# A two-layer graph network on one core: first layer from gathered bf16 rows of h, sums kept by span, products of zeros on TensorE

## The chip, the core and the metric

The kernel runs on one core of a Trainium2 chip. A core has TensorE (PE), VectorE (DVE), ScalarE (ACT), GpSimd (POOL) and SyncE (SP), each with its own queue, and 16 DMA engines. The metric is the device time of one execution in microseconds.

## The reference

`x` is 12500 nodes by 64. There are 212500 edges, sorted by target; `src`, `dst`, a type of 16 and 8 attributes each.

```python
h = relu(layernorm(x))
# layer one: 16 relations
msg = sum_r (h[src] * (etype == r)) @ weight[r]
x = x + segment_sum(msg, dst)
h = relu(layernorm(x))
# layer two: W1 is 136 x 64, W2 is 64 x 64
m = relu(concat(h[src], h[dst], attr) @ W1 + b1) @ W2 + b2
x = x + segment_sum(m, dst)
```

## The kernel before

Nodes are held as 98 blocks of 128 (`x3`, resident in SBUF). Edges are cut into tiles of 128, four tiles to a group: 1661 tiles with edges, 416 groups. As edges are sorted, the targets of a group lie in a window of `W` = 64 nodes that starts at the group's first target.

**Front** (lines 143 to 236). `x` is loaded in stretches of 16 blocks over SP and ACT in turn (line 111). Several tables are derived from `dst`, `src` and the types (lines 169 to 209), among them `flag`, which says whether the sorted path may be taken; with the data used here it is. Then `layer_norm` (lines 131 to 137) runs over 14 blocks at a time, PE transposes (L216) and multiplies each node's h with all 16 matrices (L223), DVE and ACT evict (L234, L235), and SP stores `rel_rows`, 1024 floats per node (L236).

**Layer one** (loop at line 351, in `in_order`). Per group, `gather` (L278) issues on POOL one indirect DMA per tile: 128 rows of 64 floats from `rel_rows`, at index source x 16 + type, into one of 8 buffers `rows_of`. `targets` (L289) lets DVE build a one-hot of each edge's place in the window. `add_sums` multiplies rows and one-hots on PE into the PSUM tile `pa` (L310, two buffers) and DVE adds it into `acc` at the window's column (L312); `acc` holds the sums of all nodes as columns. The windows' columns are loaded into registers for eight groups at a time (L298). When a span of four blocks can get no more sums (`finished`), `second_products` transposes it (L327), adds it to `x` (L328), normalises, and stores two tables: `a_rows` (h times the first 64 rows of W1) and `b_rows` (h times the next 64 rows, plus b1) (L349).

**Layer two** (loop at line 377). It needs all of `a_rows`. Per group POOL gathers `a_rows[src]`; SP loads the group's window of `b_rows` (L391, 64 rows, above 8 rows of W1) and its attributes (L394, under the one-hot); ACT builds a transposed one-hot of the targets by `relu(1 - |dst - w|)` (L396, L402); one f32 product per tile gives b and attribute terms (L405); DVE adds the gathered rows (`z`, L407), ACT applies relu (`hid`, L409), and `add_sums` runs again with a 65th row of ones for b2. `results` multiplies a finished span with W2 (L367), adds `x` (L369) and stores.

The order within each engine is that of the program, as the tile framework emits it; an engine that waits holds everything queued behind it.

Of the kernel before, what the change touches and what calls it, by code (L numbers as in the profile page):

```python
# [37 lines left out]
P = 128  # L38
# [7 lines left out]
NB = -(-N // P)  # L46
NT = 1664
# [5 lines left out]
G = 4  # L53
W = 64
# [4 lines left out]
BS = 4  # L59
GS = 17  # L60
SLACK = 2
NCHK = (NGR - SLACK) // GS
RG = 8

# [18 lines left out]
def gnn_kernel(  # L83
    ctx: ExitStack, tc, x, src, dst, etype, attr, src_t, dst_t, typ_t, attr_t, first, last, w_rel, w1, b1, w2, b2, out
# [7 lines left out]
    rel_rows = dram.tile([NB * P, R * D], F32, name="rel_rows")  # L92
    a_rows = dram.tile([NB * P, D], F32, name="a_rows")
    b_rows = dram.tile([NW, D], F32, name="b_rows")
    rel_table = rel_rows.rearrange("n (r d) -> (n r) d", r=R)
# [12 lines left out]
    XL = 16  # L108
    for i, b0 in enumerate(range(0, NB - 1, XL)):
        b1_ = min(b0 + XL, NB - 1)  # L110
        (nc.sync, nc.scalar)[i % 2].dma_start(
            x3[:, b0:b1_, :], x[b0 * P : b1_ * P].rearrange("(b p) d -> p b d", p=P)
        )
    nc.scalar.dma_start(x3[:tail, NB - 1, :], x[(NB - 1) * P :])
    flag = keep.tile([1, 1], I32, name="flag")
    first_row = keep.tile([1, NGR], I32, name="first_row")
    row_i = keep.tile([P, NT], I32, name="row_i")
    src_i = keep.tile([P, NT], I32, name="src_i")
    local = keep.tile([P, NT], F32, name="local")

    neg_w = keep.tile([W, NGR], F32, name="neg_w")
    none_row = float((NB * P - 1) * R)

    def layer_norm(pool, b0, nb, name):

        st = pool.tile([P, nb, 6], F32, name=f"{name}_st")
        mv = pool.tile([P, nb, 2], F32, name=f"{name}_mv")
        rs = pool.tile([P, 2, nb], F32, name=f"{name}_rs")
        h = pool.tile([P, nb, D], F32, name=f"{name}_h")
        for k in range(nb):  # L130
            V.bn_stats(st[:, k, :], x3[:, b0 + k, :])  # L131
        for k in range(nb):
            V.bn_aggr(mv[:, k, :], st[:, k, :])
        S.activation(rs[:, 0, :], mv[:, :, 1], AF.Sqrt, bias=eps, scale=1.0)  # L134
        V.reciprocal(rs[:, 1, :], rs[:, 0, :])
        for k in range(nb):
            V.tensor_scalar(
                h[:, k, :], x3[:, b0 + k, :], mv[:, k, 0:1], rs[:, 1, k : k + 1], op0=ALU.subtract, op1=ALU.mult
            )
        return h  # L140


    with ExitStack() as c1:
# [3 lines left out]
        ps3 = c1.enter_context(tc.tile_pool(name="p1ps3", bufs=3, space=PSUM))  # L147

        wrel = big.tile([P, R, D], F32, name="wrel")
        for k in range(2):  # L150
            nc.scalar.dma_start(wrel[k * D : (k + 1) * D], w_rel.rearrange("r i o -> i r o"))


        seq = big.tile([P, NT], I32, name="seq")
        nxt = big.tile([P, NT], I32, name="nxt")
        nc.sync.dma_start(seq, dst[:EP].rearrange("(p j) -> p j", p=P))
        nc.sync.dma_start(nxt, dst[1 : EP + 1].rearrange("(p j) -> p j", p=P))
        ends = big.tile([P, 2, NGR], I32, name="ends")
        nc.scalar.dma_start(ends[:, 0, :], first.unsqueeze(0).to_broadcast([P, NGR]))
        nc.scalar.dma_start(ends[:, 1, :], last.unsqueeze(0).to_broadcast([P, NGR]))  # L160
        nc.scalar.dma_start(first_row, first.unsqueeze(0))
        nc.sync.dma_start(src_i, src_t)
        typ_i = big.tile([P, NT], I32, name="typ_i")
        nc.sync.dma_start(typ_i, typ_t)
        dst_i = big.tile([P, NT], I32, name="dst_i")
        nc.sync.dma_start(dst_i, dst_t)

        bad = big.tile([P, NT + NGR + NCHK], F32, name="bad")
        V.tensor_tensor(bad[:, :NT], nxt, seq, op=ALU.is_lt)
        ends_f = big.tile([P, 2, NGR], F32, name="ends_f")  # L170
        V.tensor_copy(ends_f, ends)
        V.scalar_tensor_tensor(
            bad[:, NT : NT + NGR], ends_f[:, 1, :], -float(W), ends_f[:, 0, :], op0=ALU.add, op1=ALU.is_ge
        )
        want = big.tile([P, NCHK], F32, name="want")
        G_.iota(
            want, pattern=[[BS * P, NCHK]], base=BS * P, channel_multiplier=0, allow_small_or_imprecise_dtypes=True
        )

        at = ends_f[:, 0, GS + SLACK :: GS]  # L180
        nchk = at.shape[1]
        V.memset(bad[:, NT + NGR :], 0.0)
        V.tensor_tensor(bad[:, NT + NGR : NT + NGR + nchk], at, want[:, :nchk], op=ALU.is_lt)
        sums = big.tile([P, 2], F32, name="sums")
        V.memset(sums[:, 1:2], 1.0)
        V.tensor_reduce(sums[:, 0:1], bad, axis=AX.X, op=ALU.add)
        pf = ps1.tile([1, 1], F32, name="hT_p")
        T.matmul(pf, lhsT=sums[:, 0:1], rhs=sums[:, 1:2], start=True, stop=True)
        V.tensor_copy(flag, pf)

        ok = big.tile([P, NT], F32, name="ok")
        typ_f = big.tile([P, NT], F32, name="typ_f")
        V.tensor_copy(typ_f, typ_i)
        V.tensor_scalar(ok, typ_f, 0.0, None, op0=ALU.is_ge)
        V.scalar_tensor_tensor(ok, typ_f, float(R), ok, op0=ALU.is_lt, op1=ALU.mult)
        V.scalar_tensor_tensor(typ_f, src_i, float(R), typ_f, op0=ALU.mult, op1=ALU.add)
        V.scalar_tensor_tensor(typ_f, typ_f, -none_row, ok, op0=ALU.add, op1=ALU.mult)
        V.tensor_scalar(row_i, typ_f, none_row, None, op0=ALU.add)  # L200
        V.tensor_tensor(
            local.rearrange("p (g k) -> p g k", k=G),
            dst_i.rearrange("p (g k) -> p g k", k=G),
            bc(ends_f[:, 0, :], 2, G, [P, NGR, G]),
            op=ALU.subtract,
        )
        row_w = big.tile([W, 1], F32, name="row_w")
        G_.iota(row_w, pattern=[[0, 1]], base=0, channel_multiplier=1, allow_small_or_imprecise_dtypes=True)
        V.tensor_scalar(neg_w, ends_f[:W, 0, :], row_w, -1.0, op0=ALU.add, op1=ALU.mult)

        LB = 14
        for b0 in range(0, NB, LB):
            h = layer_norm(wk, b0, LB, "r")
            for b in range(0, LB, 2):
                hT_p = ps1.tile([P, P], F32, name="hT_p")
                T.transpose(hT_p, h[:, b : b + 2, :].rearrange("p k d -> p (k d)"), ident)  # L216
                hT = wk.tile([P, P], F32, name="hT")
                S.activation(hT, hT_p, AF.Relu)  # L218
                pr = [ps3.tile([P, R * D], F32, name="pr") for _ in range(2)]
                half = R * D // 2  # L220
                for j in range(2):
                    for k in range(2):
                        T.matmul(  # L223
                            pr[k][:, j * half : (j + 1) * half],
# [16 lines left out]
    def in_order():  # L241
        with ExitStack() as c2:
# [20 lines left out]
            for t in bwin:  # L263
                nc.scalar.dma_start(t[W:, :], w1[2 * D :])
# [557 lines left out]
```

## Time and profile before

| | |
|---|---|
| median of 11 runs | 5148.47 us (5140.68 to 5157.12) |
| profiled execution | 5147.21 us, span 5145.3 us |
| busy | PE 1814.5, DVE 837.3, ACT 753.4, POOL 3143.2 us |
| first gather, last gather of layer one | 243.5 us, 2593.4 us |
| first gather of layer two, last | 2612.3 us, 5116.5 us |

In a group line of the profile, "x1661 | 1571.2, 946 | 1021.4" is 1661 instructions, 1571.2 us busy, 946 ns each, 1021.4 us of idle time just before them. "remote" is a signal whose sender the profile doesn't name, "issue" is time in which nothing visible was waited for. The granted clock is TensorE's share of its full clock. An f32 matmul shows as two records.

### The profile page before, as it was taken

The numbers are of one execution on the slowest core, as the hardware profiler recorded it, in microseconds if no ns is written. First come the engines' busy times: TensorE is split into PE (matmuls) and PEld (weight loads), VectorE is DVE, ScalarE is ACT, GpSimd is POOL, SyncE is SP. The second block draws the span as 40 slices with busy tenths as digits, with TensorE's granted clock in tenths as the row PEclk, the third lists the DMA queues.
The fourth block names the chain that finished last, engine by engine and source line by source line (L and its number), as shares of the span: only waits on it lengthen the run. The fifth ranks groups of instructions, "written<-read, shape, count | busy, mean of one in ns | idle before, by whom it ended". The sixth has DMA issues, their size and how long they took to land. (4 is left out here: it accounts for less than half of the span.)

```text
span 5145.3 us, 37992 instructions
## 1 busy us (share of the span) xinstructions
PE 1814.5 (35%) x10948; PEld 1598.3 (31%) x10948; DVE 837.3 (16%) x2995; ACT 753.4 (15%) x1575; POOL 3143.2 (61%) x3331
## 2 busy tenths in 40 slices
PE   4522122212122112222135444444445444444445
PEld 1211111111121112111124444444444444444445
DVE  5411111111111111111111111111111111111111
ACT  2300000000000000000012222222222222222222
POOL 0066666666666666666656666666666566666665
PEclk9855555555555555555555555555555555555555
DMA  6611111111111111111112222222222232222222
GB/s 227 258 25 27 26 25 27 26 26 27 26 26 28 25 26 28 26 25 27 25 34 46 53 45 52 55 46 54 45 56 50 45 60 47 52 45 54 53 45 43
DMA packets 219120, 249.35 MB, mean 48 GB/s; under 512 B 145655, under 2 KB 145912, under 8 KB 215576
## 3 DMA queue, kind: packets, MB, share of 16 engines
q0 software_dynamic: 106304, 109.07, 11.4%
q1 hardware_dynamic: 103282, 135.08, 9.7%
q10 hardware_dynamic: 9318, 2.69, 0.3%
q8 instruction: 91, 1.49, 0.1%
q14 instruction: 125, 1.02, 0.1%
HBM read 185.55 MB, written 61.02 MB: 48 GB/s over the span
## 5 line engine op out<-in xcount | busy, mean ns | idle before, releaser
L278 POOL DMA_INDIRECT rows_of<-rel_rows,row_i x1661 | 1571.2, 946 | 1021.4 <-issue 415.9
L278 POOL DMA_INDIRECT rows_of<-a_rows,src_i x1661 | 1570.9, 946 | 952.1 <-issue 469.7
L310 PE MATMUL pa<-oh,rows_of 128*64 128x64 f32 x3322 | 434.4, 314 | 1419.4 <-DVE acc L312 702.4
L405 PE MATMUL pab<-bwin,ohT 72*128 72x64 f32 x3322 | 794.5, 421 | 286.8 <-issue 118.3
L405 PEld LDWEIGHTS pab<-bwin,ohT 72*128 72x128 f32 x3322 | 753.4, 332 | 299.2 <-remote 100.7
L310 PEld LDWEIGHTS pa<-oh,rows_of 128*64 128x64 f32 x3322 | 371.3, 217 | 1484.1 <-DVE acc L312 721.6
L310 PE MATMUL pa<-oh,hid 128*65 128x64 f32 x3322 | 459.7, 319 | 952.1 <-ACT hid L409 771.4
L310 PEld LDWEIGHTS pa<-oh,hid 128*65 128x65 f32 x3322 | 405.3, 229 | 985.2 <-ACT hid L409 794.2
L312 DVE TENSOR_TENSOR acc<-acc,pa 64x64 f32 (+1 forms) x832 | 178.5, 215 | 3142.5 <-remote 2426.2
L402 ACT ACTIVATE ohT<-off 64x512 f32<-64x512 f32 x416 | 253.9, 620 | 838.6 <-issue 402.1
L289 DVE TENSOR_TENSOR oh<-local,iota_p 128x256 f32<-128x256 f32 x832 | 338.1, 407 | 44.0 <-remote 43.0
L409 ACT ACTIVATE hid<-z 128x256 f32<-128x256 f32 x416 | 169.1, 408 | 1042.1 <-DVE z L407 800.7
L396 ACT ACTIVATE off<-dst_bc,neg_w 64x512 f32<-64x512 int32 x416 | 282.6, 708 | 15.1 <-DMA dst_bc<-in_dst 12.5
L407 DVE TENSOR_TENSOR z<-pab,rows_of 128x256 f32<-128x256 f32 x416 | 173.3, 421 | 664.7 <-remote 342.0
L134 ACT ACTIVATE s_rs<-s_mv,eps 128x4 f32<-128x4 f32 (+1 forms) x25 | 7.4, 297 | 1762.4 <-DVE s_st L131 1086.0
L223 PE MATMUL pr<-wrel,hT 64*128 64x512 f32 x392 | 111.1, 690 | 69.9 <-ACT hT L218 69.9
L339 PE MATMUL pab<-w1ab,hT 64*128 64x128 f32 x196 | 40.3, 498 | 227.4 <-issue 146.7
L339 PEld LDWEIGHTS pab<-w1ab,hT 64*128 64x128 f32 x196 | 25.6, 308 | 236.0 <-issue 151.0
L367 PE MATMUL pT<-w2b,acc 65*128 65x64 f32 x196 | 48.0, 426 | 106.2 <-DVE acc L312 87.0
L234 DVE COPY rows<-pr 128x512 f32<-128x512 f32 x98 | 63.8, 685 | 97.6 <-issue 75.0
L367 PEld LDWEIGHTS pT<-w2b,acc 65*128 65x128 f32 x196 | 44.0, 329 | 109.6 <-DVE acc L312 89.4
L235 ACT COPY rows<-pr 128x512 f32<-128x512 f32 x98 | 57.7, 588 | 130.2 <-DVE rows L234 113.1
(57 smaller groups left out, 350.0 us busy)
## 6 DMA issues: line engine op xcount, KB each, us to landing
dst_bc<-in_dst SPq DMA_DIRECT2D x52, 1024.0 KB
rel_rows<-rows SPq DMA_DIRECT2D x49, 1024.0 KB
rows_of<-rel_rows,row_i POOLq DMA_INDIRECT x1661
rows_of<-a_rows,src_i POOLq DMA_INDIRECT x1661
ohT<-in_attr_t SPq DMA_DIRECT2D x416, 16.0 KB
bwin<-b_rows SPq DMA_DIRECT2D x416, 16.0 KB
a_rows<-ab SPq DMA_DIRECT2D x24, 128.0 KB
b_rows<-ab SPq DMA_DIRECT2D x24, 128.0 KB
```

The lines of the kernel that those rows point to most:

```text
L223: T.matmul(pr[k][:, j * half : (j + 1) * half], lhsT=hT[k * D : (k + 1) * D, :], rhs=wrel[k * D : (k + 1) * D, j * R // 2 : (j + 1) * R // ...
L278: G_.indirect_dma_start(out=t[:, i, :], out_offset=None, in_=table, in_offset=bass.IndirectOffsetOnAxis(ap=idx[:, k : k + 1], axis=0),)
L289: V.tensor_tensor(oh[:, :n, :], bc(local[:, g * G : g * G + n], 2, W, [P, n, W]), bc(iota_p, 1, n, [P, n, W]), op=ALU.is_equal,)
L310: T.matmul(pa[:rows], lhsT=lhs(i), rhs=oh[:, i, :], start=(i == 0), stop=(i == n - 1))
L312: V.tensor_tensor(to, to, pa[:rows], op=ALU.add)
L339: T.matmul(pab.rearrange("p s d -> p (s d)"), lhsT=hT[i * D : (i + 1) * D, :], rhs=w1ab[i * D : (i + 1) * D].rearrange("i k o -> i (k o)") ...
L367: T.matmul(po[:, k, :], lhsT=acc[:, (b0 + k) * P : (b0 + k + 1) * P], rhs=w2b, start=True, stop=True)
L396: S.activation(off, dst_bc[:, (g % RG) * G * P : (g % RG + 1) * G * P], AF.Abs, bias=neg_w[:, g : g + 1],)
L402: S.activation(ohT[:W, :], off, AF.Relu, bias=1.0, scale=-1.0)
L405: T.matmul(pz[:, i, :], lhsT=ohT[:, i * P : (i + 1) * P], rhs=bw, start=True, stop=True)
L407: V.tensor_tensor(z[:, :n, :], pz[:, :n, :], a_of[:, :n, :], op=ALU.add)
L409: S.activation(r[:, :n, :D], z[:, :n, :], AF.Relu)
```

## The change

**Front.** The table of relations and its products go. Instead each node's relu(h) is split into three bf16 parts (together about 24 bits) and stored as a row of 192 bf16, `h_rows`. `x` comes on SP alone, in eight uneven chunks; GpSimd takes the two subtractions of the split. The tables that need whole passes over the edges move into the loop of layer one, in eight parts (`load_part`, `codes`).

**Layer one.** A tile's gather takes 128 rows of `h_rows`, at the source alone, into one of 12 buffers (as in layer two). ACT builds per tile a one-hot over 16 relations x 12 places (a window of `WT` = 12 nodes per tile), in bf16. Six bf16 products per tile (three parts, two halves of the relations) give sums of h by relation and node, and DVE adds them per tile into a table that covers a span of two blocks and 128 nodes ahead; two such tables take turns. When a span is done, `finish` multiplies its table with the 16 matrices (eight f32 products of 128 x 128 by 64 per block) and goes on as `second_products` did; its steps are spread over the following tiles. The last two blocks are finished one by one. `b_rows` is stored as three bf16 parts.

**Beside it.** `attributes` splits the edge attributes into bf16 parts for layer two, in DRAM.

**Layer two.** Windows have 40 nodes, the one-hots and both operands of the products at L405 are bf16: 120 rows of b parts, and 72 rows of attributes against `w1c_9`. `prepare`, `hidden` and `add_up` run for three successive groups at a time. Sums lie in two span tables.

**Products of zeros.** `keep_busy` issues bf16 products of a zero tile, 512 columns wide: two after each tile of layer one but the last few groups, seven in `prepare` and seven in `add_up` of layer two.

The core of the diff:

```diff
-W = 64
+W = 40
+WT = 12
+FRONT = (6, 14, 14, 14, 14, 14, 12, 10)
+FILL_N = 512
+FILL1 = 2
+FILL2 = 14
...
+        def rows_of_sources(b0, nb):
+            h = layer_norm(wk, b0, nb, "r")
+            parts = wk.tile([P, nb, 3, D], BF16, name="parts", bufs=3)
+            rest = wk.tile([P, nb, D], F32, name="rest")
+            S.copy(parts[:, :, 0, :], h)
+            G_.tensor_tensor(rest, h, parts[:, :, 0, :], op=ALU.subtract)
+            S.copy(parts[:, :, 1, :], rest)
+            G_.tensor_tensor(parts[:, :, 2, :], rest, parts[:, :, 1, :], op=ALU.subtract)
+            nc.sync.dma_start(
+                h_rows[b0 * P : (b0 + nb) * P, :].rearrange("(b p) c -> p b c", p=P),
+                parts.rearrange("p b k d -> p b (k d)"),
+            )
...
+        for k, nb in enumerate(FRONT):
+            rows_of_sources(sum(FRONT[:k]), nb)
+            if k == 5:
+                checks()
...
-                t = wk.tile([P, G, D], F32, name="rows_of", bufs=8)
+                t = wk.tile([P, G, width], dtype, name=f"rows{width}", bufs=12)
...
+            def relations(code, k, n):
+                off = wk.tile([P, G, RW], BF16, name="off_r")
+                oh = wk.tile([P, G, RW], BF16, name="oh_r", bufs=3)
+                for i in range(n):
+                    S.activation(off[:, i, :], iota_s, AF.Abs, bias=code[:, k + i : k + i + 1])
+                last_ins["ACT"] = S.activation(oh[:, :n, :], off[:, :n, :], AF.Relu, bias=1.0, scale=-1.0)
+                return oh
...
+            def keep_busy(idle, n):
+                for _ in range(n):
+                    product(idle, lhsT=still[:, :P], rhs=still, start=True, stop=True)
...
+            def go_on(k):
+                n = BLOCKS[k][1] * P
+                S.copy(tables[(k + 1) % 2][:, :, :AHEAD], tables[k % 2][:, :, n : n + AHEAD])
...
+                    msg, n = gather(h_rows[:, :], src_i, g, 3 * D, BF16)
+                    if n:
+                        oh = relations(code, gc * G, n)
...
+                    for i in range(n):
+                        k = gc * G + i
+                        if k % RG == 0:
+                            with behind("DVE"):
+                                at = windows(places, k, SN + AHEAD - WT, ENG.DVE)
+
+                        pa = psA.tile([P, HW], F32, name="pa", bufs=4)
+                        for j in range(3):
+                            for half in range(2):
+                                product(
+                                    pa[half * D : (half + 1) * D, :],
+                                    lhsT=msg[:, i, j * D : (j + 1) * D],
+                                    rhs=oh[:, i, half * HW : (half + 1) * HW],
+                                    start=(j == 0),
+                                    stop=(j == 2),
+                                )
+                        to = tables[STEP[g] % 2][:, :, bass.ds(at[k % RG], WT)]
+                        last_ins["DVE"] = V.tensor_tensor(
+                            to, to, pa.rearrange("p (r n) -> p r n", r=RH), op=ALU.add
+                        )
...
+                        if g <= FIN[NREG - 1]:
+                            keep_busy(idle, FILL1)
...
+                    last_ins["SP"] = nc.sync.dma_start(
+                        at9,
+                        attr_p[:, :, e0 : e0 + G * P]
+                        .rearrange("k i e -> (k i) e")
+                        .unsqueeze(0)
+                        .to_broadcast([3, 3 * EA, G * P]),
+                    )
...
+                    for i in range(n):
+                        cols = slice(i * P, (i + 1) * P)
+                        product(pz[g][:, i, :], lhsT=ohT[:, cols], rhs=bw, start=True, stop=False)
+                        product(pz[g][:, i, :], lhsT=at9[:, cols], rhs=w1c_9, start=False, stop=True)
+                    keep_busy(idle, FILL2 // 2)
...
+                        pa = ps.tile([DA, W], F32, name="pa", bufs=2)
+                        for i in range(n):
+                            product(pa, lhsT=r[:, i, :], rhs=o[:, i, :], start=(i == 0), stop=(i == n - 1))
+                        if g < FIN[NFIN - 2]:
+                            keep_busy(idle, FILL2 // 2)
```

## The prediction

> **What bounds it now.** I read the page first: its slices and its costliest groups.
>
> ```profile
> POOL 0066666666666666666656666666666566666665
> PEclk9855555555555555555555555555555555555555
> ...
> L278 POOL DMA_INDIRECT rows_of<-rel_rows,row_i x1661 | 1571.2, 946 | 1021.4 <-issue 415.9
> L278 POOL DMA_INDIRECT rows_of<-a_rows,src_i x1661 | 1570.9, 946 | 952.1 <-issue 469.7
> ```
>
> POOL does nothing for two of 40 slices, then gathers to the end: 1661 gathers in each layer, 946 ns of each busy. PE's granted clock is near full only in those first two slices. I then cut the span where the gathers of each layer begin and end (windows by stage: length, busy time per engine, clock, DMA share):
>
> ```profile
> core 0: us, PE busy (x) PEld busy (x) DVE busy (x) ACT busy (x) POOL busy (x), PEclk, DMA share, GB/s
> 0.00:243.50 243.50, 124.71 (x443) 44.17 (x443) 123.98 (x419) 65.39 (x155) 1.10 (x10) 0.93 0.67 246
> 243.50:2594.40 2350.90, 497.56 (x3622) 412.79 (x3622) 309.13 (x1276) 41.55 (x170) 1571.21 (x1661) 0.51 0.14 27
> 2594.40:2612.20 17.80, 7.50 (x43) 5.35 (x43) 6.69 (x32) 2.11 (x10) 0.00 (x0) 0.50 0.12 25
> 2612.20:5117.40 2505.20, 1165.79 (x6728) 1117.74 (x6728) 390.39 (x1246) 636.24 (x1224) 1570.92 (x1661) 0.50 0.25 50
> 5117.40:5145.30 27.90, 18.97 (x112) 18.22 (x112) 7.13 (x24) 8.10 (x17) 0.01 (x1) 0.50 0.08 17
> ```
>
> What POOL waits for in the first layer's stretch, and then in the second's:
>
> ```profile
> POOL rows_of L278 <- issue: 415.9, 1364, 0.3
> POOL rows_of L278 <- remote: 288.4, 114, 7.2
> ...
> POOL rows_of L278 <- PE pa L310: 31.8, 39, 6.9
> ```
>
> ```profile
> POOL rows_of L278 <- issue: 469.7, 1460, 4.8
> POOL rows_of L278 <- DVE z L407: 329.6, 88, 10.3
> POOL rows_of L278 <- DVE acc L312: 105.9, 33, 4.7
> ```
>
> The first line is the pace (415.9/1364 = 0.305 us between two gathers): 0.946 + 0.305 = 1.251 us each, 1661 x 1.251 = 2077.9 us a layer. The rest is standing still: 2350.9 - 2077.9 = 273.0 us in layer one, 2505.2 - 2077.9 = 427.3 us in layer two. A gather waits there for one of 8 buffers, which a matmul or an add releases. Why those are late shows in the timeline:
>
> ```profile
> 1119.96 0.95 POOL L278 DMA_INDIRECT rows_of<-rel_rows,row_i  x1 [0.30 <-issue]
> 1125.65 0.21 DVE L312 TENSOR_TENSOR acc<-acc,pa 64x64 f32 x1 [14.15 <-remote]
> ...
> 1125.88 0.95 POOL L278 DMA_INDIRECT rows_of<-rel_rows,row_i  x1 [4.98 <-remote]
> ```
>
> DVE waited 14 us for PE's signal, although PE is 21% busy in this stage: nothing is short of throughput, the signals of a sparse PE come late. In the front, at clock 0.93, DVE has no wait on "remote" in the list of waits. So the time is 243.5 front + 2077.9 + 273.0 + 17.8 + 2077.9 + 427.3 + 27.9 = 5145.3, with 1.9 outside the span 5147.2, 0.02% under the median of the 11 runs (5148.5), so no correction.
>
> **The parts of the change.** *Front (now 243.5).* The table of 1024 floats per node, its products, evictions and 51 MB store go; rows of 384 bytes (4.8 MB) remain. DVE is then the longest: bn_stats 98 x 0.134 (14 took 1.87) = 13.1, aggregates 98 x 0.072 = 7.1, subtract and scale 2 x 6272 elements at 1.125 ns (1664 took 1.87 us) = 14.1, eight reciprocals 1.8, the checks 1.9 + 0.6 + some 20 small ones at 0.19 = 6.3: 42.4 us, from 7.0 (its first start before). x comes all over SP now (49 blocks were issued in 11.6 us, so 98 in 23): ahead of DVE. Behind the last ten blocks stand two ACT copies (640 elements, 0.62 us per 512: 1.5) and two GpSimd subtracts. GpSimd elementwise work of this kind is not in the trace; 128 elements of its mask took 0.284 us, 2.2 ns each, or at DVE's 1.125: 2.8 or 1.4 us, and for all blocks 27.6 or 14 us, beside DVE's 42. I take 2.8. Last store to first gather took 5.6 before (237.9 to 243.5). Sum 7.0 + 42.4 + 4.3 + 5.6 = 59 us; 45 if DVE's operations overlap, 80 if GpSimd and DVE disturb each other by twofold.
>
> *Gathers.* Count, index and partitions stay; a row has 384 bytes instead of 256 in layer one. The 946 ns are the same for both tables and at DMA shares 0.14 and 0.25, so I keep 1.251. Bounds: 0 to +10% of layer one (208 us). Buffers go from 8 to 12 groups.
>
> *ACT, layer one, per group of 4 tiles (5.0 us of gathers).* The one-hots move here from DVE: four Abs of 192 elements between 0.283 (128) and 0.409 (256): 1.4; a Relu of 768 at 1.21 ns: 0.9; clearing 2048 and carrying 1024 elements once in 8.5 groups: 0.4; attribute copies and the rest 0.3. 3.0 of 5.0: hidden. *DVE:* four table adds of 96 elements at 0.25, 1.0; node steps, codes and attributes 0.6; window loads come fourfold as often, one per 8 tiles, each at most 1.7 us (the gap to the next add, 1128.5 to 1130.2): 0.9. 2.5 of 5.0: hidden. If that cover failed, each 0.1 us over 5.0 per group would cost 42 us a layer.
>
> *PE.* Two views of PE alone, both without gaps, at granted 1.0 and at half:
>
> ```profile
> 52.97 1.99 PE L223 MATMUL pr<-wrel,hT 64*128 64x512 f32 x8 [1.16 <-ACT hT L218]
> 1006.90 3.70 PE L310 MATMUL pa<-oh,rows_of 128*64 128x64 f32 x32 [12.19 <-DVE acc L312]
> ```
>
> An f32 product is two records; the first row's run in pairs side by side, so 0.50 us per 512-column record at full clock; the second gives 0.116 us per 64 columns at half. A bf16 zero product of 512 columns costs 0.50 (a whole f32 record) or 0.25 (half the bytes); I take 0.25. Layer one per tile at full clock: 2 zero products and 6 products of 96 columns: 0.78 to 1.56 us against 1.251. Layer two per group: 14 zero products, 8 small bf16 products and 8 f32 records at 0.058: 3.5 + 0.9 = 4.4, or 7.9, against 5.0. So PE stays under the gathers if a zero product takes under (5.0 - 0.9) / 14 = 0.29 us. The Trainium skill (TensorE: Matmul & The Clock Gate, on what gates the clock) says that a busy stretch of about 3.4 us releases the full clock and an idle one takes it back; the clocks 0.93 and 0.50 above agree. The same page has 215.7 ns for 512 bf16 columns at full and 426.7 at half clock: 3.0 + 0.9 us per group, the same forecast, or 6.0 + 1.9, PE the bound.
>
> *Late signals.* They lie in the stages at half clock and not in the front, so with PE kept at work I let 700.3 us fall to 15 (layer starts: code and window tables, covered by 12 buffers). Bounds 0 and 700. With them gone the gathers themselves are next.
>
> *Layer two's transfers.* Per group 72 KB of attributes and 15 KB of b rows; both patterns begin with a dimension of 3. The Trainium skill (DMA: Bandwidth & Descriptors, rules for kernel authors) says that such an outermost dimension keeps a transfer on that many engines, which speaks against this layout; no row here shows it. By the rows, 50 GB/s at share 0.25 is 12.5 GB/s per busy engine; were all 87 KB on three, that is 29 KB, 2.3 us, plus 0.25 x 5.0 of other traffic: 3.6 of 5.0. Hidden either way.
>
> *Boundary and end.* From the last gather: landing at most 2.8 (first gathers of layer two: the z add starts 2.8 after the fourth), product and add 0.9, eight products 1.7, then as before from the transpose to the next gather (2605.0 to 2612.3) 7.3, less the gather's own 0.95: 11.7 for 17.8. End: 2.8 + z to the store 2.8 + store to the end 5.3 + seven zero products 1.8 - 0.95 = 11.7 for 27.9.
>
> Sum: 59 + 2077.9 + 11.7 + 2077.9 + 11.7 + 1.9 + 15 = 4255 us.
>
> **The rivals.** *The signals stay late.* For it: PE is more than twice as busy in layer two (47%) and the standing still is larger. Against: the front. Half of it left: 4255 - 15 + 350 = 4590; all: 4940. *Gathers of wider rows are slower* by 10%: 4463. Against: equal 946 ns at all loads. *PE becomes the bound (slower).* The zero products stand in PE's queue ahead of the next tile's products, and every add and buffer waits for those. At half clock, or a whole f32 record each: 1.56 us x 1661 = 2591 and 7.9 x 415.25 = 3280; with 59 + 11.7 + 11.7 + 1.9: 5955. It decides from 0.29 us per zero product on. For it: the clock stood at 0.50 with PE 47% busy in layer two. Against: a PE that is never idle is what the front had most of, and its clock was 0.93.
>
> **How the numbers follow.** Gathers bound, signals on time: 0.75, at 4255 (own range 4214 to 4330: front 45 to 80, remaining waits 0 to 70, ends 6 less each). Late signals in part or whole 0.13, wider rows slower 0.04, PE bound 0.08. The range, 4205 to 4500, holds the first case, wider rows and the mild part of late signals. A measurement tells some 0.2% from no change (10 us): the first three are faster, 0.91 with 0.01 given to no change, and PE bound slower, 0.08.
>
> **What would show it.** Right: first gather near 59 us, gathers 1.25 us apart with few long waits, clock near 1.0 in both layers, PE some 62 and 88% busy. Wrong: POOL waiting on PE or DVE for hundreds of us, clock 0.5, or a gather busy for over 1 us.

## The result, and the profile after

The changed kernel takes 5302.24 us (median of 8 runs, 5291.74 to 5320.12) against 5148.47 us before: 1.0302 times, with a 95% interval of 1.029 to 1.0315. It is slower by 3%, where 4255 us were forecast. The experiments fell on seven occasions of two kinds: on five the kernel before took 5148 to 5180 us (medians), as here, and on two it took 4416 and 4413 us; times are compared only within one occasion.

The page of the changed kernel, its slices and its costliest groups (instruction count, busy time, mean ns, idle time before):

```profile
POOL 5666666666656666566456666656665566665663
PEclk9767677776767777667668888888888888888888
...
L433 PE MATMUL idle<-still 128*128 128x512 bf16 x9012 | 2965.7, 448 | 313.6 <-issue 305.9
L390 POOL DMA_INDIRECT rows<-a_rows,src_i x1661 | 1566.8, 943 | 1065.3 <-DVE oh L620 493.8
L390 POOL DMA_INDIRECT rows<-h_rows,src_i x1661 | 1584.4, 954 | 966.0 <-PE pa L433 445.0
```

POOL now works in every slice, and a gather of 384-byte rows takes what one of 256 bytes took. But the idle time before the gathers has not shrunk (1021.4 and 952.1 before, where the first figure holds the 241.8 us that POOL waited for the front; 966.0 in layer one and 1065.3 in layer two now), and the granted clock changes between half and full instead of standing at full. By stage, cut where the gathers of each layer begin and end:

```profile
core 0: us, PE busy (x) PEld busy (x) DVE busy (x) ACT busy (x) POOL busy (x), PEclk, DMA share, GB/s
0.00:69.80 69.80, 0.19 (x2) 0.09 (x2) 51.30 (x253) 16.65 (x25) 28.37 (x27) 1.00 0.58 140
69.80:2616.10 2546.30, 2086.75 (x14670) 918.24 (x14670) 561.72 (x2334) 1140.53 (x2473) 1584.43 (x1661) 0.72 0.20 45
2616.10:2669.20 53.10, 34.89 (x326) 27.97 (x326) 19.60 (x92) 27.85 (x66) 0.00 (x0) 0.50 0.05 11
2669.20:5248.30 2579.10, 1935.83 (x12291) 988.43 (x12292) 353.59 (x1347) 680.65 (x1212) 1566.85 (x1661) 0.84 0.25 56
5248.30:5296.10 47.80, 41.94 (x348) 24.69 (x346) 10.70 (x43) 13.98 (x26) 0.00 (x0) 0.97 0.06 15
```

Against the stages before (243.5, 2350.9, 17.8, 2505.2, 27.9): front -173.7, layer one +195.4, between +35.3, layer two +73.9, end +19.9; sum +150.8 us. The front gave most of what was hoped for, and everything behind it took that back and more. At 2077.9 us of gathers per layer, they stand still for 468.4 us in layer one and 501.2 in layer two, where it was 273.0 and 427.3. POOL's longest waits in each of the two:

```profile
POOL rows L390 <- PE pa L433: 445.0, 260, 2.7
```

```profile
POOL rows L390 <- DVE oh L620: 493.8, 158, 11.0
```

In layer one the releaser is again a product that reads the gather's buffer. In layer two the profile names VectorE's one-hot (L620), which doesn't read that buffer; the add `z` (L657), which does, runs on the same engine, so only the engine is to be trusted there.

### The profile page after: what moved, and what is told of

Read it like the earlier page. It is cut to its first block, busy times and chain, and to the rows that moved or that the text cites. A ratio compares the mean times of both kernels' runs of the same rounds, so it can differ in the third digit from the quotient of the medians.

```text
span 5296.1 us, 77092 instructions
## 1 busy us (share of the span) xinstructions
PE 4099.6 (77%) x27634; PEld 1959.4 (37%) x27634; DVE 996.9 (19%) x4069; ACT 1879.7 (35%) x3801; POOL 3179.7 (60%) x3349
## 4 chain that ended last, share of the span: by engine, by line
PE 73%; issue 17%; another core or an unknown queue 4%; DVE 2%; ACT 1%; POOL 1%; DMA 1%; DVEq 0%; SPq 0%; ACTq 0%; POOLq 0%
PE idle L433 46%; PE pa L433 15%; PE pT L433 8%; PE pz L433 3%; POOL rows L390 1%; PE pab L433 1%; DVE table L554 1%; ACT oh_r L404 1%; PE po L433 0%; DMA rows<-h_rows,src_i 0%; ACT off_r L403 0%; PE pab L479 0%; POOL rest L200 0%; DMA part<-in_dst_t 0%
## 5 line engine op out<-in xcount | busy, mean ns | idle before, releaser
L433 PE MATMUL idle<-still 128*128 128x512 bf16 x9012 | 2965.7, 448 | 313.6 <-issue 305.9
L390 POOL DMA_INDIRECT rows<-a_rows,src_i x1661 | 1566.8, 943 | 1065.3 <-DVE oh L620 493.8
L390 POOL DMA_INDIRECT rows<-h_rows,src_i x1661 | 1584.4, 954 | 966.0 <-PE pa L433 445.0
L433 PEld LDWEIGHTS <-still 128*128 128x128 bf16 x9012 | 901.7, 117 | 1101.2 <-issue 671.0
L433 PE MATMUL pa<-oh_r,rows 128*64 128x96 bf16 x9966 | 662.3, 245 | 253.0 <-issue 145.9
L433 PEld LDWEIGHTS <-rows 128*64 128x64 bf16 x9966 | 388.4, 127 | 1250.0 <-issue 1187.7
L554 DVE TENSOR_TENSOR table<-table,pa 128x96 f32 x1661 | 422.4, 254 | 1897.9 <-PE pa L433 1260.3
L404 ACT ACTIVATE oh_r<-off_r 128x768 bf16<-128x768 bf16 x416 | 349.9, 841 | 1143.1 <-PE pa L433 855.3
L403 ACT ACTIVATE off_r<-iota_s,code 128x192 bf16<-128x192 f32 x1661 | 627.6, 443 | 7.1 <-issue 1.7
L433 PE MATMUL pT<-wrel,table 128*128 128x64 f32 x1568 | 465.9, 393 | 55.2 <-issue 33.3
L657 DVE TENSOR_TENSOR z<-pz,rows 128x256 f32<-128x256 f32 x416 | 172.1, 414 | 29.6 <-issue 18.0
```

The source lines that it names most:

```text
L390: G_.indirect_dma_start(out=t[:, i, :], out_offset=None, in_=table, in_offset=bass.IndirectOffsetOnAxis(ap=idx[:, k : k + 1], axis=0),)
L403: S.activation(off[:, i, :], iota_s, AF.Abs, bias=code[:, k + i : k + i + 1])
L404: last_ins["ACT"] = S.activation(oh[:, :n, :], off[:, :n, :], AF.Relu, bias=1.0, scale=-1.0)
L433: last_ins["PE"] = T.matmul(*args, **kw)
L554: last_ins["DVE"] = V.tensor_tensor(to, to, pa.rearrange("p (r n) -> p r n", r=RH), op=ALU.add)
L657: last_ins["DVE"] = V.tensor_tensor(z[:, :n, :], pz.pop(g)[:, :n, :], a_of.pop(g)[:, :n, :], op=ALU.add)
```

## Experiments

The stages of the kernels that carry the argument, in us, each from its own profiled execution. The rows come from four occasions, on which the kernel before took 5148 (the first two rows), 5180, 5179 and 4416 us. In the first two rows a layer is cut at the end of its last gather, in the others at its start, 0.9 us earlier:

| kernel | front | layer one | between | layer two | end |
|---|---|---|---|---|---|
| before | 243.5 | 2350.9 | 17.8 | 2505.2 | 27.9 |
| changed | 69.8 | 2546.3 | 53.1 | 2579.1 | 47.8 |
| without zero products | 69.7 | 2473.0 | 54.0 | 2544.8 | 39.3 |
| the same, 5 buffers | 69.7 | 2477.2 | 28.3 | 2559.4 | 14.9 |
| the same program, where before takes 4416 | 69.4 | 2085.9 | 13.8 | 2074.3 | 11.1 |

### Are the zero products the cost?

Four kernels: no zero products, those of layer one alone, those of layer two alone, and all of them with data instead of zeros.

```diff
-FILL1 = 2
-FILL2 = 14
+FILL1 = 0
+FILL2 = 0
```

> The changed kernel with no zero products at all (both counts 0). Theory A, the zero products make TensorE the bound: the layers fall to the gathers' pace of 1.251 us a tile, 2078 to 2200 us each in place of 2546 and 2579, and the whole to 4350 to 4500 us. Theory B, signals of a sparse TensorE are late and the zero products only replaced that loss by their own: the layers stand still as in the kernel before (273 and 427 us over the pace), the whole is near 4950 us; if the late signals are worse for the new, finer steps, up to 5300.

> Zero products in layer one alone (two per tile), none in layer two. Theory A: layer one stays at 2546 us, layer two falls from 2579 to 2078 to 2200, the whole 4800 to 4920 us. Theory B: layer two falls only to some 2505, the whole 5150 to 5230 us.

> Zero products in layer two alone (14 per group), none in layer one. Theory A: layer one falls from 2546 to 2078 to 2200, the whole 4850 to 4950 us. Theory B: layer one stays near 2350, the whole near 5100 us.

```diff
-            V.memset(still, 0.0)
+            S.copy(still, x_sb[:, :FILL_N])
```

> The changed kernel, but the tile of the filling products holds the first 512 columns of x in bf16 in place of zeros; the products' results are not used, as before. If the clock's monitor counts what the operands toggle, the granted clock rises from 0.78 toward 1.0, TensorE needs about 1.0 us a tile, and the whole falls toward 4400 us. If it counts instructions alone, or the clock falls for another reason, clock 0.78 and 5300 us stay.

The kernel before took 5180.17 us beside them (the changed kernel as it is did not run on this occasion). Without zero products: 5185.8 us, 1.001 times before (1.0 to 1.002). Layer one's alone: 5269.13, 1.0177 (1.0146 to 1.0207). Layer two's alone: 5254.88, 1.013 (1.0112 to 1.0149). With data: 5360.89, 1.0339 (1.0315 to 1.0362), at a granted clock of 0.777, not above the 0.782 of the zeros. So the zero products cost time wherever they stand (75 us of layer one, 2548.5 against 2473.0), and data in their place did not raise the clock. They are not the cause: without any of them the layers still stand 395 and 467 us over the gathers' pace, 162 more in sum than in the kernel before (273 and 427, on an occasion on which that kernel took 32 us less). The theory that they had made TensorE the bound, and that all would be well without them, fell.

### Are the gathers the cause?

```diff
-                    G_.indirect_dma_start(
-                        out=t[:, i, :],
-                        out_offset=None,
-                        in_=table,
-                        in_offset=bass.IndirectOffsetOnAxis(ap=idx[:, k : k + 1], axis=0),
-                    )
+                    nc.sync.dma_start(t[:, i, :], table[(k % NB) * P : (k % NB + 1) * P, :])
```

(from the kernel without zero products; most of SyncE's other transfers inside the layers go to GpSimd, those of every group in layer two stay on SyncE)

> The kernel without zero products, with each gather replaced by a plain read of 128 neighbouring rows, issued by SyncE; the few other transfers of SyncE in the layers go to GpSimd. The indices are left out, so GpSimd works out no descriptors for the rows; TensorE, VectorE and ScalarE do what they did. Theory A (GpSimd's gathers, or what they do to the memory or to the signals, make TensorE's signals late): the pauses of 0.70 us per TensorE instruction vanish, a tile of the first layer takes well under 1.25 us, and the two layers together take under 3600 us against 5018 without this edit. Theory B (the ring of TensorE, VectorE and ScalarE is late by itself, the gathers only hide half of it): the pauses stay, the layers stay at 2400 to 2550 us each, total 5050 to 5200.

It took 3179.4 us, beside a kernel before of 5158.23 (one run each). From its first table add to its last a tile of layer one takes 0.851 us, a tile of layer two 0.988, where the gathers' own pace is 1.25 and the kernel with gathers needed 1.49 and 1.53. Its page has the slices of the clock, and layer one's add with its idle time:

```profile
PEclk9955555555555555555555555555555555555555
...
L549 DVE TENSOR_TENSOR table<-table,pa 128x96 f32 x1661 | 421.1, 254 | 678.1 <-PE pa L428 524.6
```

This row of clocks is like that of the kernel before, half throughout the layers. VectorE waits 678.1 us ahead of its adds, in a layer that is over in 1412 us, and no wait for `pa` there is longer than 2.3 us. TensorE at half clock, with the same work per tile, sends its signals in time as soon as no gather runs.

### TensorE beside gathers, by itself

After the front, instead of the layers (those are left out), TensorE does the same work three times: 500 products of 512 columns, 300 times the six small products of a tile, and 300 such tiles with VectorE's add out of four PSUM tiles.

```diff
+                    keep_busy(idle, 500)
+                    for _ in range(300):
+                        small(pb)
+                    for _ in range(300):
+                        pa = ps.tile([P, HW], F32, name="pa", bufs=4)
+                        small(pa)
+                        V.tensor_tensor(acc, acc, pa, op=ALU.add)
```

> The front, and then instead of the layers three times the same work for TensorE: 500 zero products of 512 columns, 300 sets of the six small products of a first-layer tile, and 300 such sets each added up by VectorE out of four PSUM tiles (the ring). First alone, then beside 300 gathers, then beside 600 plain reads by SyncE; the layers themselves are left out. Theory A (the gathers cause the pauses): alone the 500 take about 110 us at a full clock, the small sets 0.25 to 0.4 us each and the ring under 0.8 us per tile, without pauses; beside the gathers the ring takes over 1.2 us per tile and the steps of 0.70 us show. Theory B (TensorE's own doing: clock or sparse work): all three rounds look alike, with pauses in the ring of each.

Windows of this run: the first row is 1000 products alone, the second the tiles with adds alone, the third the stretch of the 300 gathers, the fourth 500 products beside plain reads.

```profile
74.00:292.00 218.00, 217.95 (x999) 98.37 (x1000) 1.22 (x5) 0.73 (x3) 0.00 (x0) 1.00 0.05 11
344.40:451.40 107.00, 94.74 (x1809) 57.45 (x1804) 75.23 (x297) 0.00 (x0) 0.00 (x0) 1.00 0.01 3
455.70:848.90 393.20, 99.38 (x232) 23.22 (x230) 0.00 (x0) 0.00 (x0) 301.99 (x300) 0.53 0.18 38
1088.00:1196.00 108.00, 108.00 (x499) 48.82 (x498) 2.13 (x27) 0.00 (x0) 0.00 (x0) 0.99 0.43 98
```

Alone a product takes 218/1000 = 0.218 us and a tile with its add 107/300 = 0.357 us. Beside the gathers 232 products went through in 393 us, 93 of them in the first 20 us; they wait for nothing in the program, and the profile puts all of TensorE's idle time down to "issue". Beside twice as many plain reads it was 0.216 again. The tiles with adds did not meet the gathers, since the 500 products held them back. The timeline shows how the gathers' stretch begins:

```profile
474.23 1.89 PE L433 MATMUL idle<-still 128*128 128x512 bf16 x8
...
481.85 0.59 PE L433 MATMUL idle<-still 128*128 128x512 bf16 x1 [1.00 <-issue]
...
483.25 0.10 PEld L433 LDWEIGHTS <-still 128*128 128x128 bf16 x1 [2.69 <-issue]
...
484.64 0.11 PEld L433 LDWEIGHTS <-still 128*128 128x128 bf16 x1 [1.29 <-issue]
485.35 0.58 PE L433 MATMUL idle<-still 128*128 128x512 bf16 x1 [0.80 <-issue]
```

For 20 us after the first gather (455.75) products run without a gap; then one instruction, a weight load or a product, passes every 0.70, 1.40 or 2.10 us (483.25, 484.64, 485.35). I call these the steps of 0.70 us. In the changed kernel's layer two they show as well: of the 1103 times that more than 0.45 us lie between two of TensorE's instructions, 466 are 0.69 to 0.71 us. With few zero products or none the instructions come in bursts and the step is hardly to be seen; that the waits on "remote" and "issue" there have the same source is argued from what follows, not seen. The granted clock goes down at 481.6, some 5 us after the steps begin, so here it follows the idle time and does not cause it.

A second such kernel asks whether the gathers have to be running for this:

```diff
+                for k in range(200):
+                    t = fetch(k, src_i)
+                V.tensor_copy(late[:, : 3 * D], t)
+                for _ in range(500):
+                    product(idle, lhsT=late[:, :P], rhs=late, start=True, stop=True)
```

(then 1000 zero products beside 200 gathers, and 1000 beside 200 plain reads issued by GpSimd; the layers are left out)

> The front and then, instead of the layers, three stages: 200 gathers with TensorE idle, and 500 products of 512 columns that wait for the last gather; 1000 zero products beside 200 gathers; 1000 zero products beside 200 plain reads that GpSimd issues. Theory A (the gathers leave something behind that has to drain, and TensorE stands in that line): where pauses show at all, the first products after the last gather pause for 15 to 30 us though no gather runs any more. Theory B (the descriptors' making itself holds TensorE up): the products after the last gather run at 0.216 us at once, those beside the gathers pause; the plain reads of the third stage pause them as the gathers do if it is the making of descriptors, and not if it is the indices. Where the kernel before takes 4416 us no stage pauses in either.

The timeline around the last gather and the products that waited for it:

```profile
321.41 1.09 POOL L712 DMA_INDIRECT got<-h_rows,src_i  x1 [0.30 <-issue]
...
324.60 11.42 PE L433 MATMUL idle<-late 128*128 128x512 bf16 x44 [274.93 <-issue]
...
338.61 0.10 PEld L433 LDWEIGHTS <-late 128*128 128x128 bf16 x1 [2.70 <-issue]
340.01 0.58 PE L433 MATMUL idle<-late 128*128 128x512 bf16 x1 [2.42 <-issue]
```

No gather runs any more, TensorE gets through 11 us of products, and then it is held in the same steps until 352 us, 30 us after the last gather. In the second stage the steps last from 475 to 732 us for gathers from 455 to 707: 3 or 4 products in 10 us instead of 46. Plain reads of GpSimd, one per 0.536 us, hold nothing up, though they go through the same software queue (q0) in as many packets of the same size (6400 of 1538 bytes for 200 reads, as for 200 gathers). So the gathers leave something that drains 25 to 30 us behind them, and TensorE stands in that line; GpSimd's issuing of transfers and the number of packets alone are not it. What drains, no run shows.

### Occasions without the steps

A third such kernel, with gathers of 128, 64 and 32 rows, plain reads and gaps between them, was to find which gathers do it; three variants of the change were to tell a limit of rate from lateness: PSUM tiles 20 instead of 4 and more buffers on all rings (a first form of this one, with six one-hot groups, did not fit into SBUF), one bf16 part of three, and 5 gather buffers.

```diff
-                        pa = psA.tile([P, HW], F32, name="pa", bufs=4)
+                        pa = banks[turn % 5][:, turn // 5 % 4, :HW]
```

> The front and then, instead of the layers, TensorE runs zero products of 512 columns without a break (0.216 us each at a full clock when nothing else runs) while GpSimd issues six blocks of 100 transfers with additions of its own between the blocks: gathers of 128 rows back to back, the same with an addition of about 1.2 us after each, gathers of 64 rows, of 32 rows, plain reads of 128 neighbouring rows, and gathers of 128 rows with an addition of about 2.8 us after each. The layers are left out. Theory A (GpSimd's making of descriptors, or its back-to-back gathers, starves TensorE): the pauses show in the first block from about 20 us in, as in the run of stages, fewer or none where the gathers are half or a third as dense, fewer rows per gather help in proportion; between the blocks the products come every 0.216 us again. Theory B (any indirect gather pauses TensorE, whatever its rate): the loss per gather is the same, about 1.2 us, in all blocks of 128 rows, so that the products' rate during the blocks with additions is 50% and 70% of the full one.

> The kernel without zero products, with more buffers between the engines: the first layer's PSUM tiles 20 instead of 4, its one-hot groups 5 instead of 3; in the second layer PSUM tiles 4 and 8 instead of 3 and 2, one-hots 8 instead of 5, ReLU tiles 8 instead of 4. Theory A (TensorE's instructions come through no faster beside the gathers, a limit of rate): the layers stay within 2% of 2473 and 2545 us, total 5130 to 5250. Theory B (each signal is late by 1 to 3 us but TensorE has the time; the ring is too short): with up to five times the tiles in flight each layer falls towards the gathers' pace of 2078 us, total 4350 to 4800.

```diff
-                        for j in range(3):
+                        for j in range(1):
```

> The kernel without zero products, with only the first of the three bf16 parts multiplied in the first layer: 2 products per tile instead of 6; the second and third part of h are left out. The gathers and all else stay. Theory A (each TensorE instruction passes at a limited rate beside gathers, and that sets the pace): the first layer falls from 2473 towards the gathers' own 2078 us, below 2250. Theory B (the gathers give up time to every instruction, but a few ns each: before, after and the runs without zero products fit about 1.37 us per tile and 6 ns per instruction of any engine): 8 instructions fewer per tile bring about 80 us, the first layer 2380 to 2420 us. The second layer stays at 2545 in both.

```diff
-                t = wk.tile([P, G, width], dtype, name=f"rows{width}", bufs=12)
+                t = wk.tile([P, G, width], dtype, name=f"rows{width}", bufs=5)
```

> The kernel without zero products, with 5 instead of 12 buffers for the gathered groups in both layers. In the run without zero products the adds lag 67 us behind their gathers in both layers, which is all 12 buffers full. Theory A (the engines behind the gathers set the pace throughout, so that depth only means lag): the layers stay at about 2473 and 2545 us, the lag falls to 25 to 30 us, the 54 us between the layers to 25 to 33 and the end from 39 to 20 to 28, total 5125 to 5160 where the run without zero products had 5186. Theory B (the depth bridges stalls of the engines behind): the layers grow by more than 40 us together and the total stays or rises.

None of the questions was answered, since the kernel before took 4416.24 us here and no step of 0.70 us showed: the products of the first came 0.22 us apart on average in every block that they reached, and the variants took 4251.4, 4249.8 (one run each) and 4255.75 us (the last 0.9635 times before, 0.9619 to 0.9651). But it gave something better, the same program in both conditions. POOL's waits with 5 buffers, first where the kernel before took 5179, then where it took 4416:

```profile
POOL rows L390 <- issue: 888.0, 2873, 5.2
POOL rows L390 <- DVE sums L675: 334.2, 102, 8.6
POOL rows L390 <- remote: 291.8, 134, 2.6
```

```profile
POOL rows L390 <- issue: 888.9, 2917, 0.3
POOL rows L390 <- DMA rows<-a_rows,src_i: 50.0, 164, 0.3
```

The pace is the same (888 us of 0.3 us each); the waits for buffers are gone, and in layer one an add starts 3.1 us after its gather instead of 25.6 (medians); this distance is called the lag below.

The two open questions were put once more, on the kernel with 5 buffers: one part, all six products made twice, and zero products of 64 columns.

```diff
-                        for j in range(3):
+                        for j in (0, 1, 2, 0, 1, 2):
```

> The change without zero products, with 5 buffers, and with only the first of the three bf16 parts multiplied in the first layer (2 products per tile instead of 6; the second and third part of h are left out). First layer with all three: 2477 us where the kernel before takes 5180. Theory A (the gathers' pace beside other work is some 1.37 us per tile, and every instruction of any engine adds about 6 ns, which is what before with 7.3 instructions per tile at 1.415 us, without zero products 20.7 at 1.489 and the change 24.5 at 1.532 fit): 8 instructions fewer give 2390 to 2405 us. Theory B (TensorE sets the pace with what it has per tile): below 2250. Where the kernel before takes 4416 us, 2078 to 2090 in both.

> The same with the six products of a tile made twice over (12 products per tile, the sum started anew the second time). Theory A: 12 instructions more of 6 ns, first layer 2590 to 2610 us. Theory B: the tile's products cost twice as much, first layer over 2900. Where the kernel before takes 4416 us, 2080 to 2100 in both.

```diff
-                    product(idle, lhsT=still[:, :P], rhs=still, start=True, stop=True)
+                    product(idle[:, :D], lhsT=still[:, :P], rhs=still[:, :D], start=True, stop=True)
```

> The change with 5 buffers and zero products in the first layer alone, two per tile as in the change, but of 64 columns instead of 512. Two of 512 columns per tile cost 75 us in the first layer (2548 against 2473). Theory A (the number of instructions counts, not their length): 50 to 80 us again, first layer 2525 to 2560. Theory B (TensorE's time counts): an eighth of the columns costs under 20 us, first layer 2477 to 2497. Where the kernel before takes 4416 us, 2080 to 2100 in both.

Again the kernel before took 4413.4 us beside them, and they took 4250.58, 4252.98 and 4255.52 (one run each): the price of an instruction where the steps show stays unmeasured. The second one settles another thing, though. Its windows of the two layers:

```profile
69.90:2153.80 2083.90, 1583.45 (x21676) 1243.54 (x21676) 580.05 (x2402) 1152.72 (x2529) 1578.10 (x1660) 0.51 0.26 56
2167.70:4240.00 2072.30, 674.84 (x6828) 607.96 (x6828) 380.57 (x1383) 701.80 (x1236) 1566.59 (x1660) 0.50 0.31 70
```

Granted clock 0.51 and 0.50, gathers running, and the layers take 2083.9 and 2072.3 us: a low clock delays nothing here.

### The whole once more, and the best version

> The changed kernel as it is, on another occasion, beside the kernel before. In the last runs the kernel before took 4416 us, not 5150 to 5180, no step of 0.70 us showed in the layers, and the variant without zero products and with 5 buffers took 4256. Theory A (the pauses beside the gathers alone made my forecast wrong): where the kernel before takes about 4416, the changed one takes 4250 to 4270 as forecast, ratio 0.962 to 0.967, with layers of 2075 to 2095 us; where the kernel before takes 5150 to 5180, it takes 5290 to 5330 again. Theory B (the zero products themselves are too much): it takes over 4300 also where nothing pauses.

> The change without its zero products, beside the two kernels. Theory A: where the kernel before takes about 4416, 4248 to 4260 and within 0.3% of the changed kernel, since the zero products then cover a low clock that does not show; where before takes 5150 to 5180, 5180 to 5195. Theory B: more than 40 us faster than the changed kernel in both.

> The change without its zero products and with 5 buffers of gathered groups instead of 12. Where the gathers pause TensorE (before at 5150 to 5180): theory A (the engines behind the gathers set the pace, depth is only lag) 5125 to 5160, by 25 to 30 us less between the layers and 12 to 18 less at the end; theory B (depth bridges stalls) at or above the run with 12 buffers. Where nothing pauses: 4256, as in the first run.

> The changed kernel as it is, once more. Theory A (without pauses its TensorE keeps up, even where the clock is low for a time): where the kernel before takes 4413 to 4416 us, 4250 to 4265, ratio 0.962 to 0.967. Theory B (at the low clock two zero products of 0.43 us each beside a tile's six are more than the gathers' 1.25 us leave): over 4300 there, with gathers waiting for pa. Where the kernel before takes 5150 to 5180, 5290 to 5390 again in both, and nothing is told apart.

Beside a kernel before of 5179.42 us the changed one took 5367.59 (1.0378, 1.0348 to 1.0407), without zero products 5190.66 (1.0025, 1.0013 to 1.0036), and with 5 buffers as well 5152.06 (0.9952, 0.9938 to 0.9966). The last is the fastest version where the steps show, and in both conditions it is faster than the kernel before, by 0.5% and 3.7%. By the profiled executions (that with 12 buffers was the slowest of its ten runs, 11 us over their median), the gain over 12 buffers is 25.5 us between the layers (53.8 to 28.3) and 23.8 at the end (38.6 to 14.8), and both layers stay within 2 us: with 12 buffers the lag is 67.5 us, with 5 it is 25.6, and it has to be worked off where a layer ends. The last run was to show the changed kernel where nothing pauses; it fell beside a kernel before of 5155.51 (5303.35, 1.0288, 1.0271 to 1.0306), so that was never seen.

## Why the prediction was wrong, point by point

**The step that failed is "Late signals".** It let 700.3 us of standing still fall to 15, and 469 + 501 = 970 were measured. It took the low clock for the cause because the signals came late in the stages at half clock and not in the front. But the front differs in at least two things, the clock and the absence of gathers, and the profile of before never shows one without the other. The runs part them: low clock and no gathers (plain reads, clock 0.53) is fast, low clock and gathers without steps (six products made twice, 0.51) is fast, gathers at a clock mostly full (changed kernel, 0.84 in layer two) stand still for 501 us. The kernel before says it most plainly: its mean granted clock was 0.52 to 0.53 on every occasion, and it took 4416 us on one and 5148 on another, 732 us less at the same low clock, which is about all of its 700.3 us of standing still. Where the steps show, they come with the gathers.

**Its bounds, 0 and 700, failed too.** "Late signals in part or whole" had 0.13 and ended at 4940, as if the change could only keep the old waits. The change put more instructions into TensorE's queue, which is what is held up. Zero products alone cost 101 us in layer one and 54 in layer two (2577.9 against 2476.8, 2614.4 against 2560.6; on another occasion, one layer at a time, 75 and 73), with what they add at the end 177 us of the median (5367.59 - 5190.66). Layer one is some 120 us longer than before even without them (2473.0 against 2350.9, over two occasions on which the kernel before differed by 32 us in all); that it follows the number of instructions is the obvious guess, and both tries to test it fell where nothing pauses. It stays open.

**"PE becomes the bound" had the right side and the wrong size.** TensorE carries 73% of the chain that ended last, but taking the zero products away brings 177 us, not the 1700 from 5955 to 4255. A zero product takes 0.216 us at full clock and 0.427 at half, against 0.25 and 0.50 forecast. Whether TensorE bounds the changed kernel where no steps show was never seen.

**Boundary and end, 11.7 each.** Measured 53.1 and 47.8. The step assumed that the work behind the last gather is up to date; it was 12 buffers behind. Where no steps show, so that nothing lags, it is 13.8 and 11.1, or 0.9 less each from the end of the last gather.

**Front, 59.** Measured 69.8. The term that was mis-sized is "subtract and scale 2 x 6272 elements at 1.125 ns" = 14.1: they took 13.0 + 12.7 = 25.7 us, some 2.05 ns per element. The operation itself is not dearer than taken, as two of the eight scalings show:

```profile
L173 DVE SCALAR_TENSOR_TENSOR r_h<-r_h,r_rs 128x640 f32<-128x640 f32 x1 | 1.9, 1905 | 0.0
...
L173 DVE SCALAR_TENSOR_TENSOR r_h<-r_h,r_rs 128x768 f32<-128x768 f32 x1 | 1.0, 959 | 0.0
```

The larger one took half the time, 1.25 ns per element. It met none of GpSimd's subtracts; the smaller ran beside one for 1.22 of its 1.91 us. Likewise, subtracts and scalings of 896 elements took 1.07 to 1.09 us where they met none, and 2.38 to 2.50 where they ran beside one for 1.4 us or more. At 1.2 ns per element the term would be 15 us (an estimate from these), so nearly all of the 10.8 us that the front is over is VectorE being slowed by GpSimd, which the prediction had only in its bound of 80 ("if GpSimd and DVE disturb each other by twofold"). GpSimd's subtracts took 2.1 ns per element, as taken (2.2).

**Gathers, 1.251 us each.** Right, in both layers and at both widths.

Without steps the sum holds, though for another kernel than the one forecast: the version with 5 buffers and no zero products took 4255.75 us against 4255. That is luck in part: the front is 10 us over, the layers some 9 under, the ends within 1. The structure was read rightly, and one wait was given to the wrong cause; for that version it was worth 896 us (5152.06 against 4255.75).

## What to carry to other kernels

Before a wait is written off because its cause goes, look for a stage that has the supposed cause without the other things that came with it; where the profile has none, the term belongs in the range on both sides, and a kernel that only swaps the suspect (plain reads for gathers) settles it in one run. Work that is put in to keep an engine awake stands in that engine's queue: measure the kernel without it first. More buffers ahead of a slow consumer bought no pace here, only lag, and the lag is paid at every point where all must be done.

## What the runs showed of the hardware

On the occasions on which the kernel before took 5148 to 5180 us (five of seven), back-to-back indirect gathers of GpSimd held TensorE up; in the two kernels that tried it by itself, to one instruction per 0.70 to 2.80 us, from 20 us after the first gather to 25 or 30 us after the last; plain reads by SyncE or GpSimd did not. On two occasions there was none of it, and the unchanged kernel was 14% faster (4416 against 5148). Chips 3 and 5 of the record were each met in both conditions, so it is not the chip alone. The packets of the gathers' queue took the same time with the steps and without (0.109 and 0.107 us on average, same program), and so did those that bring instructions (1.13 and 1.12 us).

What differs besides is that the trace of the same program holds 23,031 semaphore events with the steps and 75,199 without. Where TensorE is held up, the events left come at the pace of its steps: from 490 to 845 us of the first kernel with stages the trace holds 506, one per 0.70 us, where back-to-back gathers on an occasion without steps leave 128 for their landings alone in every 10 us. So the holding up and the loss of records go together; which of them brings the other, or what brings both, no run shows. As every time here comes from a recorded execution, recording itself is a rival that none of the runs excludes.

GpSimd slowed VectorE in the front: one subtract or scaling of 896 elements took 1.07 to 1.09 us alone and 2.38 to 2.50 beside a subtract of GpSimd.

The Trainium skill (TensorE: Matmul & The Clock Gate, part 1, on what gates the clock) lets a busy stretch of about 3.4 us release the full clock. In the changed kernel the clock stayed at half for 30.7 us on end, from 824.7 to 855.4 us, though TensorE was busy all that time and its matmuls began at most 0.57 us apart; here the measurement decides, and keeping TensorE busy did not keep its clock. The row of that stretch:

```profile
824.70:855.40 30.70, 30.64 (x168) 14.84 (x167) 5.12 (x21) 13.53 (x26) 18.86 (x20) 0.50 0.16 33
```
